# Seven block products through one PSUM bank: one-block evictions against two phases with one copy of the bank, with new schedule settings

## The chip, the cores and the metric

One core of one Trainium2 chip. The metric is the device time in microseconds of one execution. All timed runs here are at a granted TensorE clock of 0.994 to 1.0.

## The reference, cut to what matters

64 graphs of 256 nodes and 128 features go through four layers, each followed by a residual and a layer norm. Layer 0, a gated unit with five steps, holds nearly all that the change touches:

```python
def step(h, _):
    m_in = jnp.einsum('nm,bmd->bnd', in_matrix, h)      # in_matrix = out_matrix = adj, 256 x 256
    ...                                                  # two gates, a candidate, 128 x 128 weights
    h = (1.0 - z) * h + z * hv
# called with time_step = 5; then attention with a fixed mask, a graph attention
# with a GIN layer, and Chebyshev propagation of order 3
```

All arithmetic is fp32. The kernel treats two graphs (a pair) at a time, 32 pairs in all.

## The kernel before

The kernel doesn't write its instructions in source order. It gives a list of operations, each with what it reads and writes, to a scheduler of its own, which simulates the engines with assumed durations and then emits one fixed order per engine:

```python
class Part(Value):                      # a part of a tile that is tracked by itself
    def __init__(self, whole, name="part"):
        ...
class Schedule:
    def add(self, ways, r=(), w=(), dma=None):
        ...
        for v in op.reads:  op.before.update(dict.fromkeys(v.writers))
        for v in op.writes: op.before.update(dict.fromkeys(v.readers))
        ...
    # an operation is ready at the end of what it depends on + SEEN[engine] + LAG;
    # durations of engines other than PE are multiplied by MARGIN
```

What PE, ScalarE and VectorE really wait for is decided later, when the program is built: semaphores are then put in for each tile. In PSUM the kernel has eight tiles of 512 columns (`"PS": (512, 8)`), each called a bank here. So the scheduler's picture (parts) and the built program's waits (banks) can differ.

The product of the adjacency with two graphs is, seen in blocks of 128, a 2 x 2 matrix (graph, half of the nodes) times a 2 x 2 matrix: eight block products, or seven with sums of blocks ahead and after (the Strassen-Winograd form). `spread` does the eight as four matmuls of 256 columns. `spread7` does the seven, each 128 columns wide, by accumulating in three blocks of one bank, and evicts a block each time that one is ready:

```python
X, Y, V = (Part(t) for _ in range(3))             # blocks 0, 2, 1 of bank t, tracked apart
def copy(to, k, r, w):
    S.add([("ACT", 0.18, lambda: nc.scalar.copy(blk(o, to), blk(t, k))),
           ("DVE", 0.2, lambda: nc.vector.tensor_copy(blk(o, to), blk(t, k)))], r, w)
def plus(to, k, r, w):
    dve(0.2, lambda: nc.vector.tensor_add(blk(o, to), blk(t, k), blk(o, to)), r, w)
product(0, H(0, 0), B(0, 0), [h], [X, Y, V], start=True)
...                                                # three sums of blocks of h, on VectorE or GpSimd
copy(0, 0, [X], [o0])
product(1, s1, T(0), [p1, V], [V])
copy(3, 1, [V], [o3])
product(2, H(0, 1), B(1, 0), [h, Y], [Y])
plus(0, 2, [Y, o0], [o, o0])
product(0, s2, T(1), [p2, X], [X])
copy(1, 0, [X], [o1])
product(1, s4, B(1, 1), [p4, V], [V])
plus(1, 1, [V, o1], [o, o1])
product(0, s3, T(2), [p1, X], [X])
plus(3, 0, [X, o3], [o, o3])
product(0, H(1, 1), T(3), [h, X], [X])
copy(2, 0, [X], [o])
```

Between first and last product lie six reads of the bank by ScalarE or VectorE. There are 140 such sets (28 pairs, five steps).

## Time and profile before

| | before |
|---|---|
| time, median | 1513.89 us of 3 runs (1513.24 to 1515.22) |
| span of the profiled run | 1513.6 us |
| PE busy | 1498.1 us, 99% |
| VectorE / ScalarE / GpSimd busy | 79% / 66% / 41% |
| PE's waits that show as idle time | 8.6 us |

The prediction shows the lines of the page behind this. Three more, groups of instructions of the page, show the change's own operations. Columns: line, engine, operation, output and input, count, then busy time in us and mean ns, then idle time of the engine just before and what ended most of it.

```profile
L576 DVE TENSOR_TENSOR a<-ps,a 128x128 f32<-128x128 f32 x420 | 109.6, 280 | 106.0 <-PE ps L565 84.9
L565 PE MATMUL ps<-aTt,a 128*128 128x128 f32 x1064 | 186.6, 276 | 5.1 <-DVE a L576 3.9
L572 ACT COPY a<-ps 128x128 f32<-128x128 f32 x489 | 117.4, 272 | 88.9 <-PE ps L565 70.1
```

L565 are the seven products, L576 the additions from PSUM (three in each of 140 sets) and L572 the copies that ScalarE took. PE shows 5.1 us of idle time before this largest of the groups of products.

### The profile page before, as it was taken

The page shows a single profiled execution, that of the slowest core. Times are in us where ns is not written, and L with a number is a line of the kernel's source. Part 1 is how long each engine was busy: PE and PEld are TensorE (multiplying, and loading weights), DVE is VectorE, ACT ScalarE, POOL GpSimd, SP SyncE. Part 2 cuts the span into 40 slices and gives each one's busy share as a digit, 9 for nine tenths or more (in the row PEclk, how much of TensorE's full clock was granted, in tenths as well). Part 3 has the DMA queues.
Part 4 walks back from the last instruction along what each step waited for, and adds up shares of the span by engine and source line. Part 5 has one row for each costly group of instructions (what it writes and reads, how often), then busy time and mean ns, then how long its engine had stood idle before and what let it go on. Part 6 is the DMA issues. An engine that isn't in the chain of part 4 may idle for free.

```text
span 1513.6 us, 26330 instructions
## 1 busy us (share of the span) xinstructions
PE 1498.1 (99%) x7156; PEld 1060.8 (70%) x7156; DVE 1191.8 (79%) x3102; ACT 1006.1 (66%) x3173; POOL 626.9 (41%) x835
## 2 busy tenths in 40 slices
PE   9999999999999999999999999999999999999998
PEld 7556566767776677667676677676676666788987
DVE  7865778898889887888788878667878778789861
ACT  3444456787777676677666676665677567778974
POOL 5212233545455453445543454243444233335552
PEclk9999999999999999999999999999999999999999
DMA  6544456887888686677575776576676577678453
GB/s 195 131 82 93 98 127 137 166 174 161 171 177 171 130 163 152 135 152 163 125 162 125 157 166 132 124 153 134 128 159 133 122 157 156 124 164 173 96 120 77
DMA packets 936515, 214.39 MB, mean 142 GB/s; under 512 B 717744, under 2 KB 931888, under 8 KB 936368
## 3 DMA queue, kind: packets, MB, share of 16 engines
q1 hardware_dynamic: 936368, 212.71, 66.7%
q8 instruction: 58, 0.95, 0.3%
q14 instruction: 89, 0.73, 0.2%
HBM read 115.81 MB, written 96.80 MB: 140 GB/s over the span
## 4 chain that ended last, share of the span: by engine, by line
PE 94%; DVE 3%; ACT 1%; DMA 1%; issue 1%; SPq 0%; POOLq 0%; ACTq 0%; POOL 0%; DVEq 0%
PE ps L565 14%; PE ps L545 13%; PE ps L705 9%; PE ps L706 9%; PE ps L698 9%; PE ps L690 9%; PE ps L691 9%; PE ps L727 7%; PE ps L841 4%; PE ps L834 3%; PE ps L797 3%; PE ps L833 3%; PE ps L757 2%; DVE b L772 1%; DVE a L576 0%
## 5 line engine op out<-in xcount | busy, mean ns | idle before, releaser
L565 PEld LDWEIGHTS ps<-aTt,a 128*128 128x128 f32 x1064 | 165.5, 191 | 82.5 <-issue 56.3
L579 POOL TENSOR_TENSOR a<-a 128x256 f32<-128x256 f32 x100 | 83.0, 830 | 296.8 <-DMA a<-e 102.7
L576 DVE TENSOR_TENSOR a<-ps,a 128x128 f32<-128x128 f32 x420 | 109.6, 280 | 106.0 <-PE ps L565 84.9
L565 PE MATMUL ps<-aTt,a 128*128 128x128 f32 x1064 | 186.6, 276 | 5.1 <-DVE a L576 3.9
L708 ACT ACTIVATE a<-ps,bzrh 128x512 f32<-128x512 f32 x160 | 109.9, 687 | 109.6 <-PE ps L706 104.4
L572 ACT COPY a<-ps 128x128 f32<-128x128 f32 x489 | 117.4, 272 | 88.9 <-PE ps L565 70.1
L694 ACT ACTIVATE a<-ps,bzrh 128x512 f32<-128x512 f32 x160 | 110.0, 690 | 91.5 <-PE ps L691 74.3
L705 PE MATMUL ps<-a,w 128*128 128x512 f32 x320 | 163.6, 593 | 0.0
L706 PE MATMUL ps<-a,u5h 128*128 128x512 f32 x320 | 163.4, 592 | 0.0
L691 PE MATMUL ps<-a,w 128*128 128x512 f32 x320 | 163.4, 592 | 0.0
L698 PE MATMUL ps<-a,w 128*128 128x512 f32 x320 | 162.2, 593 | 0.0
L526 DVE STREAM_TRANSPOSE a<-a 128x512 f32<-128x512 f32 x217 | 151.1, 700 | 10.8 <-PE ps L706 2.2
L727 PEld LDWEIGHTS ps<-W,a 128*128 128x128 f32 x1024 | 135.6, 192 | 33.0 <-issue 29.2
L651 ACT ACTIVATE a<-ps 128x128 f32<-128x128 f32 x456 | 121.1, 287 | 48.2 <-PE ps L727 23.8
L659 POOL TENSOR_TENSOR s<-s,neg_half 128x4 f32<-128x4 f32 x128 | 144.4, 1128 | 9.3
L235 ACT COPY a<-ps 128x512 f32<-128x512 f32 (+1 forms) x164 | 85.2, 523 | 88.8 <-PE ps L545 59.6
L700 ACT ACTIVATE a<-ps,bzrh 128x512 f32<-128x512 f32 x160 | 109.7, 689 | 51.1 <-PE ps L698 42.3
L727 PE MATMUL ps<-W,a 128*128 128x128 f32 x1024 | 141.8, 275 | 0.0
L690 PE MATMUL ps<-a,W 128*128 128x512 f32 x256 | 131.1, 594 | 0.7 <-DVE x L673 0.7
L656 POOL TENSOR_SCALAR s<-s 128x4 f32<-128x4 f32 x96 | 30.0, 313 | 239.3 <-ACT a L651 199.4
L565 PEld LDWEIGHTS ps<-aT,a 128*128 128x128 f32 x728 | 108.4, 191 | 26.4 <-issue 20.8
L565 PE MATMUL ps<-aT,a 128*128 128x128 f32 x728 | 125.7, 276 | 0.6 <-issue 0.2
(199 smaller groups left out, 3367.9 us busy)
## 6 DMA issues: line engine op xcount, KB each, us to landing
e<-a SPq DMA_DIRECT2D x279, 256.0 KB
a<-e SPq DMA_DIRECT2D x1116, 64.0 KB
e<-b SPq DMA_DIRECT2D x29, 512.0 KB
b<-e SPq DMA_DIRECT2D x116, 128.0 KB
x<-x_in SPq DMA_DIRECT2D x32, 256.0 KB
t<-xT_in SPq DMA_DIRECT2D x32, 256.0 KB
a<-d SPq DMA_DIRECT2D x32, 256.0 KB
y_out<-a SPq DMA_DIRECT2D x32, 256.0 KB
```

What stands on the lines that cost most here:

```text
L526: dve(n / 512 * 0.55 + 0.09, lambda: nc.vector.transpose(st.at(n), i.at(n)), [i], [st])
L545: nc.tensor.matmul(t.at(2, N)[:, b, :], tokens(i)[:, 2 * b + j, :], right.ap[:, j, :], start=(b == j == 0), stop=(j == 1), skip_group_chec ...
L565: pe(mm(128), lambda: nc.tensor.matmul(blk(t, k), left(), rt(), start=start, stop=True, skip_group_check=True), [*r, right, terms], w)
L572: S.add([("ACT", 0.18, lambda: nc.scalar.copy(blk(o, to), blk(t, k))), ("DVE", 0.2, lambda: nc.vector.tensor_copy(blk(o, to), blk(t, k)))] ...
L651: nc.scalar.activation(tokens(junk)[:, c, :], v.at(len(tiles), D)[:, k, :], AF.Square, scale=D ** -0.5, accum_out=mv()[:, c, 1:2])
L659: pool(1.02, lambda: nc.gpsimd.tensor_tensor(rs(), rs(), neg_half.ap, op=ALU.pow), [s, neg_half], [s])
L690: nc.tensor.matmul(t.at(512), mat("u3"), hT.at(512), start=True, stop=False)
L691: nc.tensor.matmul(t.at(512), w4.ap, mT.at(512), start=False, stop=True)
L698: pe(mm(512), lambda t=t, mT=mT: nc.tensor.matmul(t.at(512), w3.ap, mT.at(512), start=False, stop=True, skip_group_check=True), [w3, mT, t ...
L705: nc.tensor.matmul(t.at(512), w5.ap, mT.at(512), start=True, stop=False)
L706: nc.tensor.matmul(t.at(512), u5h.ap, r.at(512), start=False, stop=True)
L727: nc.tensor.matmul(tokens(t)[:, c, :], tokens(i)[:, c, :], w(), start=(first and k == c == 0), stop=(k == len(lefts) - 1), skip_group_chec ...
```

## The change

The intent: fewer hand-overs of the bank between PE and the evicting engines. Four products go to the four blocks of the bank, one copy takes the bank out, three more products add to what is in the bank, and two reads finish. The sums of 128 columns are joined into sums of 256 where they can be. With it come new settings of the schedule: which layouts are turned by DMA (`BY_DMA`), which pairs use seven products (the last two now also do, so 150 sets), when pairs come due, the preferences between engines (`SPARE`), the assumed delay between engines (`LAG`, 0.8 to 0.3 us), and the numbers of buffers.

```diff
-BY_DMA = {"h": 0, "y": 2, "x1": 3, "x2": 2, "w": 3, "z": 2, "x3": 0}
+BY_DMA = {"h": 1, "y": 0, "x1": 0, "x2": 3, "w": 0, "z": 3, "x3": 0}
-FIRST, FINAL = 2, 2
+FIRST, FINAL = 2, 0
-"X": (512, 14), ... "H": (520, 5)          # cut from CLASSES, the numbers of buffers
+"X": (512, 15), ... "H": (520, 6)
-SPARE = {"DVE": 0.6, "DVE+": 1.0, "POOL": 0.4}
+SPARE = {"DVE": 0.6, "DVE+": 0.0, "POOL": -0.3}
-DUE, LAST_DUE, LAST = 30.0, 9.0, 8
+DUE, LAST_DUE, LAST = 15.0, 12.0, 12
-MARGIN, LAG = 1.06, 0.8
+MARGIN, LAG = 1.1, 0.3
-HOLD = (0.0, -40.0, 0.0, 60.0)
+HOLD = (0.0, -20.0, 0.0, 40.0)
 ...  in spread7: the products and evictions printed above are replaced by
+product(0, H(0, 0), B(0, 0), [h], start=True)       # every product now declares the whole bank t
+product(1, s1, T(0), [p1])
+product(3, s3, T(2), [p1])
+product(2, s2, T(1), [p2])
+evacuate(lambda: o.at(512), lambda: t.at(512), [t], [o])
+sum_(0.335, 0.8, lambda e: e.tensor_add(sv.at(4, P)[:, 0:2], o.at(4, P)[:, 0:2], o.at(4, P)[:, 2:4]), [o], [p1])
+product(0, H(0, 1), B(1, 0), [h])
+product(3, H(1, 1), T(3), [h])
+product(1, s4, B(1, 1), [p4])
+sum_(0.2, 0.46, lambda e: e.tensor_add(blk(o, 3), blk(sv, 0), blk(sv, 1)), [p1], [o])
+evacuate(lambda: blk(o, 0), lambda: blk(t, 0), [t], [o], (0.17, 0.2))
+dve(0.335, lambda: nc.vector.tensor_add(o.at(4, P)[:, 1:3], t.at(4, P)[:, 1::2],
+                                        blk(sv, 0)[:, None, :].to_broadcast([P, 2, P])), [t, p1], [o])
```

More of the change, by code (lines that the diff above doesn't have):

```diff
@@ L37 @@
 ROWS = ["l1_bias", "bp", "b1", "gat_g", "gat_b", "b2"]
-CLASSES = {"X": (512, 14), "T": (512, 4), "A": (512, 30), "H": (520, 5), "B": (1024, 5), "S": (32, 64), "PS": (512, 8), "D": (512, 4), "E": (1024, 8)}
+CLASSES = {"X": (512, 15), "T": (512, 4), "A": (512, 30), "H": (520, 6), "B": (1024, 5), "S": (32, 64), "PS": (512, 8), "D": (512, 4), "E": (1024, 8)}
 SEEN = {"PE": 0.23, "ACT": 0.16, "DVE": 0.16, "POOL": 0.12, "SP": 0.0}
@@ L550, in spread7 @@
     def spread7(h, right, terms):
-        sv, t, o = Value("A", name="sums"), Value("PS", name="ps"), Value("A", name="mT")
+        sv, o, t = Value("A", name="sums"), Value("A", name="mT"), bank()
         p1, p2, p4 = (Part(sv) for _ in range(3))
-        X, Y, V = (Part(t) for _ in range(3))
-        o0, o1, o3 = (Part(o) for _ in range(3))
-        blk = lambda v, k, n=1: v.at(512)[:, k * P:(k + n) * P]
+        blk = lambda v, k: v.at(512)[:, k * P:(k + 1) * P]
         H = lambda b, j: lambda: blk(h, 2 * b + j)
@@ L562, in spread7, with product @@
         s3, s1, s2, s4 = (lambda k=k: blk(sv, k) for k in range(4))
-        def product(k, left, rt, r, w, start=False):
+        def product(k, left, rt, r, start=False):
             pe(mm(128), lambda: nc.tensor.matmul(blk(t, k), left(), rt(), start=start, stop=True, skip_group_check=True),
-               [*r, right, terms], w)
+               [*r, right, terms, *[t] * (not start)], [t])
         def sum_(us, us_pool, fn, r, w):
             S.add([("DVE+", us, lambda: fn(nc.vector)), ("POOL", us_pool, lambda: fn(nc.gpsimd))], r, w)
-        def copy(to, k, r, w):
-            S.add([("ACT", 0.18, lambda: nc.scalar.copy(blk(o, to), blk(t, k))),
-                   ("DVE", 0.2, lambda: nc.vector.tensor_copy(blk(o, to), blk(t, k)))], r, w)
-        def plus(to, k, r, w):
-            dve(0.2, lambda: nc.vector.tensor_add(blk(o, to), blk(t, k), blk(o, to)), r, w)
-        product(0, H(0, 0), B(0, 0), [h], [X, Y, V], start=True)
         sum_(0.335, 0.8, lambda e: e.tensor_sub(sv.at(4, P)[:, 0:2], h.at(4, P)[:, 0::2], h.at(4, P)[:, 2:4]), [h], [p1])
@@ L581, in spread7 @@
         sum_(0.2, 0.46, lambda e: e.tensor_add(s4(), s2(), H(0, 1)()), [h, p2], [p4])
-        copy(0, 0, [X], [o0])
-        product(1, s1, T(0), [p1, V], [V])
-        copy(3, 1, [V], [o3])
-        product(2, H(0, 1), B(1, 0), [h, Y], [Y])
-        plus(0, 2, [Y, o0], [o, o0])
-        product(0, s2, T(1), [p2, X], [X])
-        copy(1, 0, [X], [o1])
-        product(1, s4, B(1, 1), [p4, V], [V])
-        plus(1, 1, [V, o1], [o, o1])
-        product(0, s3, T(2), [p1, X], [X])
-        plus(3, 0, [X, o3], [o, o3])
-        product(0, H(1, 1), T(3), [h, X], [X])
-        copy(2, 0, [X], [o])
+        product(0, H(0, 0), B(0, 0), [h], start=True)
[11 more added lines that the diff above has]
+                                                blk(sv, 0)[:, None, :].to_broadcast([P, 2, P])), [t, p1], [o])
         return o
```

## The prediction

> **What bounds the kernel now.** I read the page from the top: the busy shares, the slices, then the chain of work that ended last.
>
> ```profile
> span 1513.6 us, 26330 instructions
> PE 1498.1 (99%) x7156; PEld 1060.8 (70%) x7156; DVE 1191.8 (79%) x3102; ACT 1006.1 (66%) x3173; POOL 626.9 (41%) x835
> ...
> PE   9999999999999999999999999999999999999998
> ...
> PE 94%; DVE 3%; ACT 1%; DMA 1%; issue 1%; SPq 0%; POOLq 0%; ACTq 0%; POOL 0%; DVEq 0%
> ```
>
> PE is busy in every slice and carries 94% of the chain. A busy PE need not be a full one, so I looked next at how densely it streams. The chain in order of time gives the start and length of unbroken runs of matmuls:
>
> ```profile
> 224.66 1.79 PE ps L727 x16
> ...
> 274.14 3.46 PE ps L545 x16
> ...
> 46.88 0.86 PE ps L705 x2
> ```
>
> Each fp32 matmul leaves two records (L705 has 160 instructions in the program and x320 in the trace), so x16 are eight matmuls. One of 128 columns therefore takes 1.79/8 = 0.223 us, one of 256 columns 3.46/8 = 0.432, one of 512 columns 0.86. Now count the instructions of the program and multiply: 1816 of 128 columns x 0.223 = 405; 864 of 256 x 0.432 = 373; 800 of 512 x 0.863 = 690 (0.86 to 0.87 in the chain); 128 of 130 columns at about 0.228 = 29. The sum is 1498 us, which is the busy time on the page. So PE really streams back to back at its own rate for the whole span. What is left of 1513.6 is 15.5 us. The waits of PE tell where:
>
> ```profile
> PE ps L565 <- DVE a L576: 3.9, 9, 1.2
> PE ps L295 <- DVE ones L293: 1.2, 1, 1.2
> PE ps L545 <- DMA a<-e: 1.2, 1, 1.2
> PE ps L565 <- ACT a L572: 1.0, 3, 0.6
> PE ps L690 <- DVE x L673: 0.7, 1, 0.7
> ```
>
> The columns are total wait, times, longest. With three more of 0.2 these make 8.6 us, of which 4.9 are before products of the seven (L565), waiting for evictions by VectorE or ScalarE, and 1.2 is the start. The rest is the end, in the windows:
>
> ```profile
> 1490.00:1500.00 10.00, 10.00 (x48) 8.81 (x47) 1.09 (x2) 4.30 (x19) 2.37 (x4) 1.00 0.36 79
> 1500.00:1513.60 13.60, 7.21 (x31) 5.36 (x30) 1.28 (x3) 5.43 (x25) 2.67 (x5) 0.97 0.21 58
> ```
>
> After the length of the stretch the first number is PE's busy time. Its last matmul ends near 1507.5, and then 6.1 us remain for the last statistics, POOL's power, the scaling and the store.
>
> [...]Here one record takes 0.223/2 = 112 ns at 128 columns and 216 at 256: small matmuls cost a few per cent more per column (0.223 x 4 = 0.89 against 0.863), no more. [...]L572, a ScalarE copy of 128 columns, takes 272 ns and L235, one of 512, 592; four small ones are 1088. [...]Here the sum of 256 columns takes 830 ns on POOL and 439 on VectorE, 1.9 times.
>
> **The change part by part.** I counted instructions in both built programs.
>
> PE's work. The products stay 7 per step, but the last two pairs now use them too: 2 x 5 steps lose 4 matmuls of 256 columns each (40 x 0.432 = 17.3) and gain 7 of 128 (70 x 0.223 = 15.6), -1.7 us. The new settings of which layouts are turned by DMA take the 128x128 transposes on PE (L520) from 60 to 40: -20 x 0.223 = -4.5 us. All else on PE is equal in count. The sum is 1491.7 against 1497.9, -6.2 us, and this lies wholly on the path that sets the end.
>
> PE's waits. Before, each set of products needs several hand-overs of its bank in a row: product, eviction of 128 columns, next product into the same block, and so on, four visits of one block. After, there is one hand-over in the middle. In the built order, PE has at least 1.31 us and in the median 2.8 us of other matmuls between the fourth and the fifth product (durations as above). What must fit in there is one copy, 0.59 us, plus the hand-overs at both ends; in the chain PE's last spread ends at 1501.52 and the matmul that reads its copy starts at 1502.18, 0.66 us later with the copy of 0.59 in it. So I expect the 4.9 us of waits of L565 to fall to about 1. After the seventh product at least 2.4 us (median 3.7) lie ahead of the first matmul that reads the result; needed is one addition of 256 columns from PSUM, about 0.41 us as L673's. The mean time from first to last product of a set, in which a bank is held, falls from 17.7 to 9.7 us of PE's work, so banks should run out less.
>
> The other engines, before to after. VectorE loses 420 additions of 280 ns, 71 copies of 283 and 41 sums (152 us in all) and gains 192 sums of 256 columns at 0.44, 57 of 128 at 0.28, 150 additions of 256 from PSUM at 0.41 and a few copies: 163 us. The new preferences of the scheduler move more to it (106 scalings at 0.32, 27 multiplications at 0.69) and some off it (49 at 0.40, copies): about +35 us in all, near 1227 us or 81%. ScalarE: 489 small copies go, 144 small and 147 large ones come, about even; with 106 and 108 fewer scalings and 98 more of another it falls by some 60 us to 63%. POOL gains 132 sums of 0.58 us less 17 of 0.83 and reaches about 700 us, 46%. All this lies beside PE's 99% and costs nothing unless it comes late.
>
> The end. Only the wait after the last matmul (6.1 us) is fixed; its operations are the same. But the last pair's way from its layer-2 product to the layer-3 matmul that reads its turned input is covered by 18.1 us of PE's work before and by 13.8 after. The trace has that way: product ends 1483.4, transpose ends 1491.5, the turned tile lands about 7 us after, 1498.5, some 15 us with 2.4 us lost behind other ScalarE work. I allow +1 us.
>
> Sum: 1491.7 of work, 1.2 start, 6.1 end, 0.6 of small gaps that I cannot place: a floor of 1499.6. Add 1 for products of the seven, 2.3 for the other waits as before, 1 at the end and 2 for new waits (below): 1506 us, 7.9 less than 1513.9, or 0.5%.
>
> **Rivals.** First, a tighter order turns into waits. The scheduler's assumed delay from one engine to the next falls from 0.8 to 0.3 us, so consumers stand closer behind producers: of PE's matmuls that depend on another engine, those with under 2 us of other matmuls since the work it all hangs on rise from 13 to 98, under 2.5 us from 71 to 259. [...]If each of the 98 lost 0.3 us it would be 29 us, 1533 in all. Second, VectorE at 81% becomes the bound in a stretch: its slices already reach 8 and 9 tenths, and it is at 28.64 of 30 us early on; 35 us over 1500 is too little to make it the bound on the whole, but it could cost 5 to 10 us, 1513. Third, PE's waits vanish altogether: 1500. Fourth, more sets in flight since the pairs now come due every 15 and not 30 us; buffers (15 and 6 in place of 14 and 5 of two kinds) may bind and show as waits on DMA; DMA's count is nearly equal, so I give this little.
>
> **Range and chances.** Faster by over 2% means under 1483.6, which is less than PE's 1491.7 of bare work: 1%, for an error in the count. Slower by over 2% means 1544, 38 us of new waits on PE: 3%. The rest, 96%, is within 2%. The range 1500 to 1515 runs from the floor to the second rival.
>
> **What would show it.** PE busy near 1492; waits of the products' line about 1 us in place of 4.9; VectorE near 1227 us, ScalarE near 947, POOL near 700; the new copy of 512 columns about 0.59 us. The prediction is wrong if PE's waits add up to over 15 us, if one line of the new products or the matmul after them waits for VectorE or POOL in many places, or if the end after the last matmul grows.

## The result, and the profile after

1494.95 us, median of 4 runs (1493.68 to 1495.75), beside 1513.98 us of 4 runs of the kernel before (1513.24 to 1515.22). The ratio is 0.9873, with a 95% interval from 0.9856 to 0.989: 1.3% faster, so within 2%, but 5 us below the low end of the predicted range. Ratios here are the mean time of one kernel's runs over that of the other's of the same rounds, so not quite the ratio of the medians.

The head of the page and the chain of work that ended last, after:

```profile
span 1493.0 us, 26228 instructions
PE 1485.7 (100%) x7196; PEld 1058.8 (71%) x7196; DVE 1227.4 (82%) x3041; ACT 974.7 (65%) x2860; POOL 701.5 (47%) x964
...
PE 100%; POOLq 0%; ACT 0%; DVE 0%; issue 0%; ACTq 0%; POOL 0%
```

VectorE took 36 us more and GpSimd 75 us more, and yet the chain, which held 3% of VectorE, is PE alone. The waits of PE, after, have a single line left (total, times, longest), which is the start of the program:

```profile
PE ps L295 <- DVE ones L293: 1.2, 1, 1.2
```

The change's groups after. L563 are the products, L235 is the evacuation (the new copy of 512 columns among other forms), L584 the new addition of 256 columns from PSUM:

```profile
L235 ACT COPY a<-ps 128x512 f32<-128x512 f32 (+2 forms) x465 | 210.8, 461 | 166.7 <-PE ps L545 48.3
L563 PE MATMUL ps<-aTt,a 128*128 128x128 f32 x1140 | 188.9, 275 | 0.0
L584 DVE TENSOR_TENSOR a<-ps,a 128x256 f32<-128x256 f32 x150 | 62.6, 418 | 70.3 <-ACT a L235 45.4
```

The idle time before the products is 0.0 where it was 5.1. One stretch of both, before and then after (length of the stretch, then busy time and count of PE, its weight load, VectorE, ScalarE and GpSimd):

```profile
100.00:1400.00 1300.00, 1293.14 (x6154) 902.83 (x6153) 1054.29 (x2711) 880.82 (x2776) 545.46 (x713) 1.00 0.70 146
```

```profile
100.00:1400.00 1300.00, 1300.00 (x6353) 920.17 (x6352) 1104.63 (x2722) 871.91 (x2560) 626.96 (x850) 1.00 0.74 148
1480.00:1493.00 13.00, 6.88 (x31) 5.40 (x29) 0.85 (x2) 4.80 (x23) 2.52 (x4) 0.95 0.15 41
```

In the same 1300 us PE was busy 6.9 us longer, 0.5%, but got 199 more matmul records done, 3.2%. (The mix isn't quite the same, so this is only a hint.) Busy time went up far less than the number of records, and the next part follows this up. The end after the last matmul, 13.0 less 6.88, is 6.1 us as before.

**Counting starts instead of busy time.** A matmul record is drawn until after the next one has started. On the page of the kernel before, a single fp32 record of 512 columns lasts 593 ns, while two of them together take 1.02 us (the first line of the timeline below):

```profile
L705 PE MATMUL ps<-a,w 128*128 128x512 f32 x320 | 163.6, 593 | 0.0
```

So a wait of PE up to about 0.16 us (593 ns less the spacing of 429.6 below) leaves no idle time, and a longer one shows that much too short. The starts have no such blur. I took from both traces the spacing from each record's start to the next one's. Undisturbed, it is 111.3 ns at 128 columns, 215.8 at 256 and 429.6 at 512, in both kernels. Call a record late when it starts over 8 ns later than that, and the sum of this its lateness. Then the span splits like this:

| us | before | after |
|---|---|---|
| PE's work (undisturbed spacing x records) | 1485.9 | 1482.1 |
| lateness before products of the seven | 12.7 | 0.0 |
| lateness elsewhere | 7.5 | 3.4 |
| first start, last record, end (1.2 + 0.2 + 6.1) | 7.5 | 7.5 |
| sum = span | 1513.6 | 1493.0 |

About 3.0 of "elsewhere" lie in the first 8 us, where records of 256 columns start 427 ns apart in place of 216, in both, at a granted clock of 1.00; I call this the warm-up, and its cause was not tested. So of 20.6 us, 3.8 are less work and 16.8 are waits that went, of which 12.7 were before products. (The execution profiled before took 1515.38 us, more than each of the four timed ones; the medians differ by 19.0.) PE's busy time contained 12.2 us that were no work before (1498.1 less 1485.9) and 3.6 after.

**What the late products waited for.** The 12.7 us are 67 late records of 38 products. For each product I looked up in the built program which semaphores it waits on and took the one that was reached last. In 34 of the 38, with 11.9 us, the last thing awaited was a read of *another* block of the same bank: 24 times VectorE's addition (9.0 us), 7 times ScalarE's copy (2.3), 3 times VectorE's copy (0.6). Reads of the block that the product itself overwrites account for 0.2 us. The timeline of the longest place, before (start, length, engine, line; in brackets idle time before and its releaser), first PE, then VectorE:

```profile
512.36 1.02 PE L691 MATMUL ps<-a,w 128*128 128x512 f32 x2
514.55 0.46 PE L565 MATMUL ps<-aTt,a 128*128 128x128 f32 x2 [1.17 <-DVE a L576]
514.85 0.40 PE L565 MATMUL ps<-aT,a 128*128 128x128 f32 x2
```

```profile
512.24 0.70 DVE L526 STREAM_TRANSPOSE a<-x 128x512 f32<-128x512 f32 x1
512.87 1.14 DVE L696 SCALAR_TENSOR_TENSOR a<-a,t 128x512 f32<-128x512 f32 x1
513.93 0.47 DVE L576 TENSOR_TENSOR a<-ps,a 128x128 f32<-128x128 f32 x2
```

PE's product at 514.55 is the fourth of a set and writes block 0. It was due at 513.22, two spacings of 0.43 after 512.36, so it was 1.33 us late, of which 1.17 show. What it waited for is the addition that reads block 2, and that stood on VectorE behind a transpose (L526; the kernel calls it a turn) and a long multiplication (L696), and ended at 514.40. For the kernel's scheduler the two have nothing to do with each other, as it tracks blocks 0 and 2 apart. The built program holds PE off the whole bank.

Why the built program guards the whole bank and not the block was not tested. What the runs show is what the guard costs when the order isn't planned for it: 11.9 us of the 12.7 here, and 17.8 of 18.7 with the new settings.

### The profile page after: what moved, and what is told of

Its sections match the earlier page's. It is cut to its first block, busy times and chain, and to the rows that moved or that the text cites.

```text
span 1493.0 us, 26228 instructions
## 1 busy us (share of the span) xinstructions
PE 1485.7 (100%) x7196; PEld 1058.8 (71%) x7196; DVE 1227.4 (82%) x3041; ACT 974.7 (65%) x2860; POOL 701.5 (47%) x964
## 4 chain that ended last, share of the span: by engine, by line
PE 100%; POOLq 0%; ACT 0%; DVE 0%; issue 0%; ACTq 0%; POOL 0%
PE ps L563 16%; PE ps L545 12%; PE ps L689 9%; PE ps L696 9%; PE ps L681 9%; PE ps L697 9%; PE ps L682 9%; PE ps L718 8%; PE ps L788 4%; PE ps L832 4%; PE ps L824 4%; PE ps L825 4%; PE ps L748 2%; PE ps L520 0%; PE ps L295 0%; PE ps L456 0%
## 5 line engine op out<-in xcount | busy, mean ns | idle before, releaser
L235 ACT COPY a<-ps 128x512 f32<-128x512 f32 (+2 forms) x465 | 210.8, 461 | 166.7 <-PE ps L545 48.3
L563 PEld LDWEIGHTS ps<-aTt,a 128*128 128x128 f32 x1140 | 167.8, 192 | 45.2 <-issue 38.0
L563 PE MATMUL ps<-aTt,a 128*128 128x128 f32 x1140 | 188.9, 275 | 0.0
L696 PE MATMUL ps<-a,w 128*128 128x512 f32 x320 | 163.6, 593 | 0.0
L582 POOL TENSOR_TENSOR a<-a 128x128 f32<-128x128 f32 x132 | 80.9, 614 | 168.1 <-DVE a L578 154.4
L563 PEld LDWEIGHTS ps<-aT,a 128*128 128x128 f32 x780 | 125.1, 191 | 42.2 <-issue 36.6
L526 DVE STREAM_TRANSPOSE a<-a 128x512 f32<-128x512 f32 x217 | 150.7, 698 | 4.8 <-PE ps L689 1.0
L718 PE MATMUL ps<-W,a 128*128 128x128 f32 x1024 | 147.1, 275 | 0.0
L563 PE MATMUL ps<-aT,a 128*128 128x128 f32 x780 | 144.9, 275 | 0.0
L650 POOL TENSOR_TENSOR s<-s,neg_half 128x4 f32<-128x4 f32 x128 | 138.6, 1083 | 8.7
L702 DVE SCALAR_TENSOR_TENSOR a<-a,a 128x512 f32<-128x512 f32 x160 | 115.1, 721 | 7.8 <-ACT a L691 6.1
L584 DVE TENSOR_TENSOR a<-ps,a 128x256 f32<-128x256 f32 x150 | 62.6, 418 | 70.3 <-ACT a L235 45.4
L570 POOL TENSOR_TENSOR a<-a,a 128x128 f32<-128x128 f32 x100 | 59.3, 593 | 119.9 <-DVE a L569 89.9
```

The source lines that it names most:

```text
L235: S.add([("ACT", us[0], lambda: nc.scalar.copy(o(), i())), ("DVE", us[1], lambda: nc.vector.tensor_copy(o(), i()))], r, w)
L526: dve(n / 512 * 0.55 + 0.09, lambda: nc.vector.transpose(st.at(n), i.at(n)), [i], [st])
L563: pe(mm(128), lambda: nc.tensor.matmul(blk(t, k), left(), rt(), start=start, stop=True, skip_group_check=True), [*r, right, terms, *[t] * ...
L650: pool(1.02, lambda: nc.gpsimd.tensor_tensor(rs(), rs(), neg_half.ap, op=ALU.pow), [s, neg_half], [s])
L696: nc.tensor.matmul(t.at(512), w5.ap, mT.at(512), start=True, stop=False)
L718: nc.tensor.matmul(tokens(t)[:, c, :], tokens(i)[:, c, :], w(), start=(first and k == c == 0), stop=(k == len(lefts) - 1), skip_group_chec ...
```

## The experiments

The main theory: the hand-overs of the old products make PE wait for reads of other blocks of the same bank, which the schedule doesn't foresee; two phases leave one hand-over, declared for the whole bank and with at least 1.31 us of other PE work in it. Rivals: the gain is from the new settings; it is from the number of small evictions, or from VectorE's load, not from the bank; it is from wrong durations in the scheduler. The letters in the expectations stand for such theories as they stood then. The runs were made on five chips, each time beside the kernel before, which took 1514.66 to 1515.6 us there (medians; 1513.98 beside the changed kernel); so times of different rows are best compared by their ratios. All results are right except where said. "Late" is the lateness as above, from each run's own trace; "products" is the part of it before products of the seven.

| run | time, us | ratio to before | late, us | products | PE work |
|---|---|---|---|---|---|
| after | 1494.95 | 0.9873 [0.9856, 0.989] | 3.4 | 0.0 | 1482.1 |
| old products, new settings | 1514.75 | 0.9999 [0.9984, 1.0014] | 23.2 | 18.7 | 1482.2 |
| new products, old settings | 1500.66 | 0.9904 [0.989, 0.9919] | 5.7 | 0.5 | 1485.9 |
| old turns | 1496.45 | 0.9876 [0.986, 0.9892] | 2.9 | 0.6 | 1484.3 |
| sums of 128 | 1496.66 | 0.9878 [0.9863, 0.9893] | 6.0 | 1.4 | 1482.1 |
| old lag | 1535.09 | 1.0136 [1.012, 1.0151] | 43.6 | 11.2 | 1482.1 |
| four copies, one hand-over | 1498.26 | 0.9892 [0.9877, 0.9906] | 7.7 | 3.7 | 1482.1 |
| four copies, four hand-overs | 1515.16 | 1.0005 [0.9988, 1.0022] | 22.5 | 2.8 | 1482.2 |
| whole bank declared, new settings (wrong) | 1539.37 | 1.0164 [1.0149, 1.0179] | 48.2 | 26.2 | 1482.1 |
| whole bank declared, old settings (wrong) | 1527.61 | 1.0087 [1.0072, 1.0102] | 32.9 | 15.0 | 1485.9 |
| two banks | 1502.88 | 0.992 [0.9905, 0.9935] | 11.8 | 7.6 | 1482.1 |
| additions out of the chain | 1505.84 | 0.9933 [0.9919, 0.9948] | 14.7 | 10.0 | 1482.1 |
| measured durations | 1514.35 | 0.9994 [0.9985, 1.0002] | 22.9 | 20.5 | 1482.2 |
| copy on VectorE | 1504.44 | 0.9924 [0.9909, 0.9939] | 12.8 | 3.6 | 1482.1 |
| VectorE loaded elsewhere | 1502.69 | 0.9916 [0.9899, 0.9932] | 11.3 | 4.3 | 1482.1 |
| layer 3 with seven, first time | 1493.59 | 0.9859 [0.9845, 0.9874] | 6.4 | 1.1 | 1476.9 |
| layers 1 and 3 with seven | 1506.53 | 0.995 [0.9933, 0.9967] | 25.5 | 11.5 | 1471.6 |
| layer 3 with seven, again | 1495.26 | 0.9867 [0.9852, 0.9882] | 9.7 | 4.1 | 1476.9 |
| after, again | 1494.65 | 0.9862 [0.9846, 0.9879] | 3.8 | 0.4 | 1482.1 |

### Structure or settings?

The changed kernel with the old body of `spread7`, and the old kernel with the new body:

```diff
-        sv, o, t = Value("A", name="sums"), Value("A", name="mT"), bank()
+        sv, t, o = Value("A", name="sums"), Value("PS", name="ps"), Value("A", name="mT")
+        X, Y, V = (Part(t) for _ in range(3))
 ...                      # and the rest of the old body in place of the new; the other run is the mirror
```

> The changed kernel with only the seven products put back as they were (one block evicted at a time, four visits of one block); all settings stay new. It has the same matmuls as the changed kernel. Theory A (the two phases took PE's waits away): the waits come back, about 12 us before products of the seven, and the time is 1505 to 1512. Theory B (the scheduler's settings took them away): about 1495, PE without waits.

Measured 1514.75 us, no gain at all, and more than theory A expected. The longest waits of PE, of this run:

```profile
PE ps L565 <- DVE a L576: 5.1, 10, 1.1
PE ps L565 <- ACT a L572: 1.7, 5, 0.4
PE ps L295 <- DVE ones L293: 1.2, 1, 1.2
```

The 3.7 us of work that the settings save are there, but lateness grew from 20.2 to 23.2. Of 18.7 us before products 17.8 ended with a read of another block: 11.1 by VectorE's additions, 6.6 by ScalarE's copies.

> The kernel before with only the two-phase products; all settings stay old. Same matmuls as the kernel before. Theory A: the waits before the products go, some 12 of the about 17 us, and the time is 1498 to 1503. Theory B: waits stay, 1510 to 1515.

Measured 1500.66 us: 14.5 less than before, with PE's work unchanged. Lateness fell from 20.2 to 5.7, which is 14.5 as well. Its waits as idle time, all of them, have no line of the products (L563):

```profile
PE ps L295 <- DVE ones L293: 1.2, 1, 1.2
PE ps L545 <- ACT x L619: 0.6, 1, 0.6
PE ps L824 <- DMA a<-e: 0.5, 1, 0.5
PE ps L748 <- DVE a L584: 0.4, 1, 0.4
PE ps L545 <- DMA x<-x_in: 0.2, 1, 0.2
PE ps L545 <- DVE a L797: 0.2, 1, 0.2
```

So the two-phase products alone bring 70 to 75% of the gain (by the ratios 0.96% of 1.27, or of 1.38 in the changed kernel's second run), and all of that is waits. The settings bring the rest, some 5 to 6 us, and only on top of the new products: 3.8 less work and some 2 of waits.

### Single parts of the change

Three parts were taken back one at a time; the other settings (`FINAL`, `SPARE`, `DUE`, `HOLD`, the buffers) were not.

```diff
-BY_DMA = {"h": 1, "y": 0, "x1": 0, "x2": 3, "w": 0, "z": 3, "x3": 0}
+BY_DMA = {"h": 0, "y": 2, "x1": 3, "x2": 2, "w": 3, "z": 2, "x3": 0}
```

> The changed kernel with the old table of which layouts are turned by DMA: 60 transposes of 128x128 on PE in place of 40. If a transpose costs what a 128-column fp32 matmul costs (0.223 us, as the prediction had it), 4.5 us longer, 1499.4; if it is one record of 0.11 us, 2.2 us longer, 1497.2, with another 1 to 3 us either way from the end of the program, which the table also changes. The trace must show the transposes' records: 60 or 120.

PE's work rose by 2.2 us, which is 20 transposes of one record of 0.111 us, and the time by 1.5. The transposes have one record each, not two: the trace of before has 28 + 24 + 8 records for 60 of them. Two of the groups with their durations (least, median, most):

```profile
L520 PE MATMUL ps<-ident,a x28: 272/273/273, 1354.8 to 1477.9; 128*128 128x128 f32 x28
...
L520 PE MATMUL ps<-ident,b x24: 272/273/273, 1412.4 to 1444.9; 128*128 128x128 f32 x24
```

Next the joined sums were split again:

```diff
-        sum_(0.335, 0.8, lambda e: e.tensor_add(sv.at(4, P)[:, 0:2], o.at(4, P)[:, 0:2], o.at(4, P)[:, 2:4]), [o], [p1])
+        for k in range(2):
+            sum_(0.2, 0.46, lambda e, k=k: e.tensor_add(blk(sv, k), blk(o, k), blk(o, k + 2)), [o], [p1])
 ...                      # the same with the last addition, from PSUM
```

> The changed kernel with the two sums of 256 columns that follow the copy split into two of 128 each. VectorE gets about 150 more instructions of PSUM (2 x 0.28 in place of 0.42, +21 us) and about 100 more of SBUF (+10 us). If the wide sums matter for PE's waits: 1498 to 1502. If only the one hand-over matters: within 2 us of 1495.

1496.66 us, at most 2 us worse than the changed kernel. The joined sums matter little.

```diff
-MARGIN, LAG = 1.1, 0.3
+MARGIN, LAG = 1.06, 0.8
```

> The changed kernel with the scheduler's old assumed delay between engines (0.8 us and a margin of 1.06 in place of 0.3 and 1.1). The number of matmuls with under 2 us of cover falls from 98 to 32. The prediction's first rival (a tighter order turns into waits) would have this one faster or equal; the trace of the changed kernel shows no waits to save, so I expect 1495 to 1500, not faster.

This missed by far: 1535.09 us, slower than before. PE's waits are spread over many lines and name transfers as often as engines:

```profile
PE ps L824 <- DMA a<-e: 4.5, 2, 3.7
PE ps L545 <- DVE x L614: 4.1, 1, 4.1
PE ps L545 <- DVE a L797: 3.0, 1, 3.0
```

In the built order only 32 matmuls have less than 2 us of cover (other matmuls between a matmul and the PE work that it hangs on, as the prediction counts it), against 98 in the changed kernel, so the looser assumption made a looser order and a slower one. The settings are tuned together, and a single one taken back lands on a bad order. Why this order runs out of work at these places I did not settle.

### Is it the number of small evictions, or of hand-overs?

Both keep the two phases and take the bank out in four copies of 128 columns. The first does so after all four products, the second after each product, which makes four hand-overs, each declared for the whole bank. One more buffer was needed.

```diff
-        evacuate(lambda: o.at(512), lambda: t.at(512), [t], [o])
+        for k in range(4):
+            evacuate(lambda k=k: blk(o, k), lambda k=k: blk(t, k), [t], [o], (0.18, 0.2))
```

> The changed kernel with the copy of the whole bank split into four copies of 128 columns, still after all four products: one hand-over, small evictions (and one more buffer of 512, without which the scheduler finds no order). ScalarE and VectorE get 600 small copies for 150 large ones, some 0.27 for a quarter of 0.59 us each, +75 us. If the number of hand-overs counts: 1495 to 1500. If the width of the evictions counts: 1503 to 1512.

1498.26 us. The 3.7 us of lateness before products are almost all before the *first* product of a set, where inputs arrive. Small evictions by themselves cost no more than the 3.3 us between the two medians.

> The same four small copies, but each right after its product, and the next product waits for it: four hand-overs in place of one, every instruction the same in number and size as in the run with four copies and one hand-over. If the number of hand-overs counts: slower than that run by 5 to 15 us, with PE's waits before the products. If it is the width or the load of the other engines: the same within 2 us.

1515.16 us, slower as expected, but not for the expected reason. Before products only 2.8 us were lost. PE's longest waits are elsewhere:

```profile
PE ps L822 <- DMA a<-e: 6.3, 1, 6.3
PE ps L545 <- DVE x L612: 2.3, 1, 2.3
PE ps L375 <- DVE a2T L459: 2.0, 1, 2.0
```

One wait of 6.3 us for a turned input of layer 3, one in the setup: a different order, that lost elsewhere. So four hand-overs in place of one, when the schedule knows of them, didn't make products wait here. And it is a warning: any edit gives a new order, and a difference of 10 us may come from somewhere else. Only lateness by place tells.

### Is it the undeclared guard of the bank?

If so, telling the old products' schedule of it might help. All of the bank is declared, in the version with new settings and in the one with old:

```diff
-        X, Y, V = (Part(t) for _ in range(3))
+        X = Y = V = t
 ...
-        product(0, H(0, 0), B(0, 0), [h], [X, Y, V], start=True)
+        t.full = True
+        product(0, H(0, 0), B(0, 0), [h], [t], start=True)
```

> The changed kernel with the old products (as in the first experiment, 1514.8 us), but the scheduler is told that each product needs the whole bank and not its block alone. Same instructions in number and size. Theory C (the waits came from a guard that the scheduler did not know of: the program makes a product wait for reads of the other blocks of its bank): PE's spacing before products 2 to 7 shows under 3 us of waits in place of 18.7, whatever the end of the program does; the time 1496 to 1510. Theory D (the small evictions and VectorE's additions themselves are too slow or too many): the waits stay, 12 us or more.

> The kernel before with that one declaration: the scheduler is told that each product needs the whole bank. Theory C: waits before the products fall from 12.7 us to under 3; time 1499 to 1510. Theory D: 1510 to 1516 with the waits still there.

Both missed: 1539.37 and 1527.61 us, with 26.2 and 15.0 us before products. Both also gave wrong values, unintended (relative errors 0.118 and 0.093): I marked the bank as fully written, though block 3 never is, which lets the scheduler reuse it as a bank preset with data. That is the likely cause; no run tested it. The times are given for what they are. Declaring the guard in this form turns a set into a chain of six hand-overs in a row, and products still wait. "Declare it and the waits go" is refuted in this simple form. The other way to test the guard is to remove what it guards together: block 0 in one bank, blocks 1 and 2 in another.

```diff
-        X, Y, V = (Part(t) for _ in range(3))
+        t2 = Value("PS", name="ps")
+        X, Y, V = t, t2, t2
 ...                      # blk(t, k) becomes blk(t2 if k else t, k) in products, copies and additions
```

> The same old products with block 0 in one bank and blocks 1 and 2 in a second bank, so what the scheduler believes and what the program guards is the same, without longer chains; it takes two banks of eight per set. Theory C: under 3 us of waits within the sets, though a lack of banks may cost elsewhere; 1497 to 1508. Theory D: 12 us of waits stay, 1510 to 1516.

1502.88 us, against 1514.75 of the same kernel with one bank: 11.9 us less. The same seven evictions and the same additions on VectorE (1227.8 us busy, against 1228.7) are still there. The waits of PE:

```profile
PE ps L566 <- DMA x<-x_in: 1.5, 3, 0.9
PE ps L566 <- DVE h L760: 1.3, 1, 1.3
...
PE ps L566 <- DVE a L577: 0.3, 1, 0.3
```

L566 are the products and L577 the additions here, and these now leave PE idle for 0.3 us where it was 5.1. Lateness that ends with a read of the product's own bank fell from 17.8 us to 3.3 (2.2 for another block, 1.1 for the same). The rest of its 7.6 us are inputs that come late and banks that aren't free yet, as each set now takes two of eight. Keep the evictions, split the bank, and most of these waits go: this is the experiment that shows the cause most directly. It does two things at once, though: block 0 no longer shares a bank with the others, and blocks 1 and 2, which still do, are now declared as one. That declaring alone doesn't do it, the runs before show.

### VectorE's part in it

First, the old products with the additions taken out of the chain on the bank: a copy by ScalarE or VectorE, and the addition afterwards from SBUF.

```diff
         def plus(to, k, r, w):
-            dve(0.2, lambda: nc.vector.tensor_add(blk(o, to), blk(t, k), blk(o, to)), r, w)
+            S.add([("ACT", 0.18, lambda: nc.scalar.copy(blk(tmp, k), blk(t, k))),
+                   ("DVE", 0.2, lambda: nc.vector.tensor_copy(blk(tmp, k), blk(t, k)))], [block], [u])
+            sum_(0.2, 0.46, lambda e: e.tensor_add(blk(o, to), blk(tmp, k), blk(o, to)), [u, r[1]], w)
```

> The changed kernel with the old products (1514.8 us, 18.7 us of waits before products), in which the three additions from PSUM[...] are replaced by copies from PSUM that ScalarE or VectorE does, and additions in SBUF beside the chain. Still one block at a time and the same visits of the blocks; ScalarE gets about 450 more small copies. Theory E (PE waits because VectorE stands in the chain from product to product): waits before products under 5 us, 1495 to 1502. Theory F (the scheduler's durations for small evictions are too short): waits stay above 12 us, 1508 to 1518.

1505.84 us, between the two theories. 10.0 us are left before products, 6.8 of them for reads of other blocks, and nearly all of these by ScalarE now:

```profile
PE ps L565 <- ACT a L572: 2.4, 6, 0.5
```

So VectorE's additions made the larger part of the waits (11.1 us with them), and the guard remains for ScalarE's copies, with about what they cost before (6.6).

Second, the assumed durations of the small evictions, 0.18 and 0.2 us, are under the measured 0.27 and 0.28. Old products, new settings, measured durations:

```diff
-            S.add([("ACT", 0.18, ...), ("DVE", 0.2, ...)], r, w)
+            S.add([("ACT", 0.27, ...), ("DVE", 0.28, ...)], r, w)
 ...                      # and 0.28 for the addition
```

> The changed kernel with the old products, and the scheduler is told the measured durations of the small evictions: 0.27 and 0.28 us in place of 0.18 and 0.2. Theory F: waits fall under 5 us, 1495 to 1503. Theory E: they shrink little, 1508 to 1516.

1514.35 us (ratio 0.9994 from 12 runs): no change, 20.5 us before products. Wrong durations are not the cause.

Third, in the changed kernel, the copy of the bank on VectorE alone, and, for comparison, as much idle work on VectorE that nothing waits for:

```diff
-        evacuate(lambda: o.at(512), lambda: t.at(512), [t], [o])
+        dve(0.61, lambda: nc.vector.tensor_copy(o.at(512), t.at(512)), [t], [o])
```

```diff
+        dve(0.61, lambda: nc.vector.tensor_add(junk.ap, h.at(512), h.at(512)), [h], [junk])
```

> The changed kernel with the copy of the whole bank on VectorE alone. VectorE's load rises by some 100 us less what the scheduler moves off it. Theory E: PE waits before the fifth product, 3 to 12 us in total, time 1499 to 1512. Theory F: the copy's listed duration is 0.61 against 0.68 measured, near the truth, so no waits there: within 3 us of 1495.

> The changed kernel with one idle addition of 512 columns more on VectorE per set, which nothing reads and no product waits for: the same load on VectorE as in the run with the copy on VectorE, but the chain from product to product stays on ScalarE. Theory E, if the place in the chain counts: no waits before the fifth product, 1495 to 1500. If VectorE's load counts: as slow as the run with the copy on VectorE.

1504.44 and 1502.69 us: by the ratios 0.5 and 0.4% slower than the changed kernel, some 8 and 6 us, with VectorE at 85 and 87%, and the lateness scattered over many lines in both. Before the fifth product, which is the one that waits for the copy, the first lost only 0.2 us. The waits of theory E there (3 to 12 us) didn't come, nor did the time of F (within 3 us of 1495); the idle work was about as slow as the copy. With a single planned hand-over it didn't matter which engine makes it. Both runs with a fuller VectorE were some 7 us slower; whether by its load or by the new order isn't separated.

### Can it be carried further?

The seven products in layer 3 as well, then in layers 1 and 3:

```diff
-        qT = to_sbuf(spread(x3, aT), "qT")
+        qT = spread7(x3, aT, aTt)
```

> The changed kernel with the seven products in layer 3 too: 32 more sets, each 7 x 0.2227 in place of 4 x 0.4316 us, -5.4 us of PE's work. If PE's streaming alone sets the time: 1489.6. VectorE gets about 1.1 us per set, +35 us, 84%: if that turns into waits, 1492 to 1500.

> The changed kernel with the seven products in layers 1 and 3 too: 64 more sets, -10.7 us of PE's work. If PE's streaming alone sets the time: 1484. With VectorE at some 86% more waits are likely: 1485 to 1496.

1493.59 and 1506.53 us. The second is above its expected 1485 to 1496. PE's work fell by 5.2 and 10.5 us, but lateness rose by 3 and 22, with VectorE at 1253.8 and 1275.3 us busy. The first was run again, on the same chip as the changed kernel:

> Seven products in layer 3 too, a second time with more rounds and beside the changed kernel: 1 to 3 us under the changed kernel of the same call. If PE's streaming alone set the time it would be 5.2 us under.

> The changed kernel itself, to compare on the same chip: 1494 to 1496.

1495.26 against 1494.65 us: no better. Nothing that I ran beats the changed kernel beyond the error.

## Why the prediction was right or wrong

**Right: the direction and the mechanism's outline.** Waits before products fell away, the end stayed at 6.1 us, and the other engines came out as counted: VectorE near 1227 (measured 1227.4), GpSimd near 700 (701.5), the addition from PSUM 0.41 (0.418). ScalarE was put at 947 and measured 974.7, which was not followed up. The new copy of 512 columns took 587 ns where 0.59 us was expected.

**Wrong: "The sum is 1498 us, which is the busy time on the page. So PE really streams back to back at its own rate for the whole span."** This is the step that failed. The two numbers agreed by accident. The work was 1485.9 us. The sum was 12.0 too high: 68 transposes (60 of L520, 8 of the setup) counted as two records of 0.111 us where they have one, 7.6; and rates taken from lines rounded to 0.01 us, such as 0.863 where the spacing gives 0.859, which over all instructions come to 4.4 (0.5 at 128 columns, 0.3 at 256, 3.0 at 512, 0.6 at 130). Two slips in the count cancel: 4 of the 864 matmuls of 256 columns are bf16, with one record of 0.109 us each (1.3 too high), and six of one column were left out (1.2 too low). The busy time was 12.2 too high, as it counts short waits as work. Two unlike errors of the same size made a proof that wasn't one. So the bare work after, put at 1491.7, was 1482.1, and PE busy, put near 1492, was 1485.7.

**Hence the floor of 1499.6 fell.** With work of 1482.1, the start and the end of 7.5 and the warm-up's 3.0, it is 1492.6, and the kernel ran in 1493.0 of span. The low end of the range was put on a wrong floor, not on a doubtful wait. The prediction also set this sum, which is a span, beside times, which are 1.8 us longer: as a time its floor is 1501.4, and the miss is that much larger. The third rival, waits vanish altogether, is what happened; only its number, 1500, was wrong.

**The term "the 4.9 us of waits of L565 to fall to about 1" was mis-sized.** It was 12.7 to 0.0. The list of waits showed 4.9 of the 12.7: about 0.16 us of each wait leaves no idle time, and most of the 67 late records were late by less than that. The reason given, several hand-overs of a bank in a row, was near; what it missed is that those hand-overs crossed blocks, so that an addition of one block held up a product into another, behind the schedule's back. The count for the first rival, 13 matmuls before with under 2 us of cover, can't have had these in it: counted over the semaphores of the built program, guard included, there are 93, and 86 of them are products of the seven.

**Less work: -6.2 predicted, -3.8 measured.** The spreads are right at -1.7; the 20 transposes are 2.2 and not 4.5.

**The allowances for new waits (+2), the end (+1) and the other waits as before (2.3) did not come.** Apart from the warm-up the changed kernel lost 0.4 us in all. The first rival, a tighter order turns into waits, is refuted: the looser order of the old lag was the one with waits. VectorE as a bound (second rival) didn't show at 82%; at 85 and 87% the kernel was some 7 us slower, in new orders. The fourth, buffers that show as waits on DMA, left no such line.

**What stays open.** Why six declared hand-overs still wait (26.2 us) when four don't (2.8): the two differ in number and in three additions that the kernel gives to VectorE alone, and I separated these only for the undeclared form. A count over the semaphores of the built programs narrows it: the products with less than 1.3 us of other matmuls between the PE work that they hang on and themselves (durations as in the prediction) are 27 before, none after and none with new products and old settings, 71 with old products and new settings, 37 with two banks, 9 with four declared hand-overs, but 90 and 43 with the whole bank declared. So the order that was built for the declared bank has little to put between its hand-overs; why the scheduler finds no more is not known. Why the old lag alone costs 40 us. Both are questions on orders, and no single operation was found that decides them.

## What to carry to other kernels

When PE seems full, check its work from start-to-start spacing and the number of records, not from busy time: here 12.2 us of PE's busy time, 0.8%, were no work, and the weight loads' busy share went from 70 to 71% while 16.8 us of waits went. Where the built program waits on PSUM by bank, as here, plan the schedule for that: reads of other blocks cost 11.9 us before and 17.8 with the new settings. If several blocks of a bank are to be evicted while others are still written, gather them into one hand-over with other matmuls in between (lateness before products went from 12.7 us to 0.5 with the old settings), or give them banks of their own (waits for the product's own bank went from 17.8 us to 3.3). Take back parts of a tuned change one by one, but read each by where the lateness is, as every edit gives a new order that can lose 10 us somewhere else.
